# Mixture-of-experts layer: results stored in the lists' own order and fetched by index in the next layer's front, row scatters in pairs

## The chip, the cores and the metric

The kernel runs on one core of a Trainium2 chip. The metric is device microseconds (us) per execution. The kernel before takes 3396.26 us, the median of 10 runs (3391.55 to 3404.77).

The core's engines work in parallel, each on its own instruction stream: PE (TensorE, matrix products; PEld are its weight loads), DVE (VectorE), ACT (ScalarE), POOL (GpSimd) and SP (SyncE, which only issues DMAs). DMAs are issued by SP and ACT in hardware queues and by POOL in a software queue; the indirect ones, which take a row index per partition, are POOL's.

## The reference

The input is one image, 256 channels of 64 x 64, so N = 4096 tokens of C = 256 numbers. Four layers follow one another: two convolution-like ones, then two transformer layers, each attention and a mixture of experts. What the change touches is layer 2's experts (hidden size 256) and the attention of layer 3, cut here to its core:

```python
def _moe(tokens, router_w, w1, b1, w2, b2):          # layer 2, 8 experts, TOP_K = 2
    logits = tokens @ router_w.T
    probs = softmax(logits, axis=-1)
    rw, re = top_k(probs, TOP_K)
    rw = rw / maximum(rw.sum(-1, keepdims=True), 1e-12)
    combine = zeros((N, E)).at[arange(N)[:, None], re].set(rw)
    out = tokens
    for e in range(E):
        h = gelu(tokens @ w1[e] + b1[e])
        y = h @ w2[e] + b2[e]
        out = out + combine[:, e:e + 1] * y
    return out
```

Layer 3 is a softmax attention over all tokens with one head of 256 (on layer-normed tokens, in this kernel's form), then experts of hidden size 1024 with the same routing.

## The kernel before

**Tokens and lists.** The tokens lie in SBUF as a tile `t` of 32 token tiles of 128 tokens; four token tiles are a block (8 blocks). For each block the router (`route_parts`) norms the tokens, finds each token's two experts and weights (`top`, `exp`, `weigh`) and its place in each expert's list (`place`, `find`), and `scatter` (L2181) writes each token's row, 260 numbers, into the DRAM buffer `xs` at both places: two indirect DMAs on POOL per token tile. The row holds the normed token and four more numbers: the token's row index and its weights, which the experts use later.

**Expert tiles.** The lists are worked off in up to 39 tiles of 256 rows (`expert_tiles`), 36 always, the rest under an If (`expert_rest`, L2400/L2402). Tiles 0 to 12 (`FULL[2]` = 13) come from table A, which is known after six blocks are routed; table B orders the others. For one tile: SP loads the rows (`expert_rows`) and the expert's weights (`expert_weights`); PE turns the rows, and ACT or DVE copies them (`f_xT`, L2376/L2377); PE multiplies by the first matrix; ACT does the gelu (`f_h`, L2456); PE multiplies by the second; DVE adds the bias (`f_y`, L2534); ACT multiplies each row by its weight (L2536); and POOL scatters the 256 rows by two indirect DMAs (L2537) into the DRAM buffer `ys`, at the token's place for its first or second expert. `expert_where` works out weight and place with five or so small DVE operations.

**What is in which order.** The second layer's attention (`attn2_sum`, 16 steps u) and the tiles up to 12 are written in a fixed order per engine (`manual_schedule`); from tile 13 on the scheduler is free. In the attention the routing of block r is spread over the steps: `scatter` of its first two token tiles at one step, of the last two at the next, and POOL's other work there is `scale` (L1734), one operation per step. The routers of the last blocks (r5, r6, r7) end inside the expert tiles: a `plan` puts pieces of them at slots ("hs", "turn", "end") of tiles 0 to 9.

**Third layer's front.** After the experts, the products of the query and key weights (`a_w_ps`, L2705, L2708) are formed; for each block, two reads of `ys` (`outputs`, L2615) on SP's and ACT's queues, two adds into `t` (`add`, L2735), the statistics (`look`, L2742 to L2746), the norm on ACT (`norm`, L2755), the turn on PE (`turn`, L2766, L2768) and the product with the joint weight matrix (`ask`, L2779). Blocks 0 to 2 go ahead of the loop. The loop runs over steps g, for each query block one per 256 keys, so two per key block: `scores` (L2843, with sums on DVE, L2830 to L2848, and the exponential on ACT, L2862), sums of the exponentials (`a_et`, L2866 to L2868, on POOL for query block 0, on DVE later), `values` (L2882), and `fetch` (a load of keys and four sums of values on POOL, L2822 to L2825). Query block 0 starts before all keys are there: in its first twelve steps the even ones add block late + 1 and turn block late, and the odd ones look, ask and norm. PE's, POOL's and DVE's order is fixed there.

```python
for g in range(first):
    late = 2 + g // 2
    more = late + 1 < NBLK
    scores(g)
    (turn, ask)[g % 2](late, 0)
    if more:
        (add, look)[g % 2](late + 1)
    if g >= LAG:
        values(g - LAG)
```

Of the kernel before, what the change touches and what calls it, by code (L numbers as in the profile page):

```python
# [10 lines left out]
F32 = mybir.dt.float32  # L11
BF16 = mybir.dt.bfloat16
I32 = mybir.dt.int32
# [44 lines left out]
CX = C + 4  # L58

# [60 lines left out]
class Net:  # L120
# [1282 lines left out]
    def attn2(self, t, S):  # L1403

        nc, tc = self.nc, self.tc
        with tc.tile_pool(name="a2", bufs=1) as pool:
# [53 lines left out]
            ahead = lambda: self.expert_rows(self.xs, S["A"]["tab"], 0, x)  # L1460
            with left:
                at["wp"] = left.enter_context(tc.tile_pool(name="a2x", bufs=2))
                at["ps"] = left.enter_context(tc.tile_pool(name="a2x_ps", bufs=1, space=PSUM))
                r6, r7 = self.attn2_sum(t, A, tri, ked, at["wp"], at["ps"], route, late, self.list_tiles(S, lent, bank, "A"), ahead)
# [9 lines left out]
            put(0, r6["place"], r6["find"], r6["weigh"], lambda: r7["turn"](0))  # L1474
            put(1, lambda: r7["turn"](1, True), lambda: r6["scatter"](range(2)), lambda: r7["move"](range(TPB)))
            put(2, r7["logits"], lambda: r6["scatter"](range(2, TPB)))
            put(3, r7["top"], r7["exp"], r7["count"])
            put(4, r7["place"], r7["find"], r7["weigh"], lambda: r7["scatter"](range(2)))
            put(5, lambda: r7["scatter"](range(2, TPB)), go)
            put(6, go)  # L1480
            put(7, go)
            put(8, go)
            put(9, go)
# [5 lines left out]
        return tiles, on  # L1489
# [229 lines left out]
    def attn2_sum(self, t, A, tri, ked, wp, ps, route, late, lists, ahead):  # L1719
# [81 lines left out]
        with self.tc.manual_schedule(engines={ET.PE, ET.DVE, ET.Activation, ET.Pool}):  # L1801
# [4 lines left out]
            for u in range(U):  # L1806
                if u + 2 < U:
                    scale(u + 2)
# [8 lines left out]
                do(u, 4, "scatter", range(0, 2))  # L1817
                do(u, 5, "scatter", range(2, 4))
# [24 lines left out]
            r5["scatter"](range(2))  # L1843
# [8 lines left out]
            r5["scatter"](range(2, TPB))  # L1852
            r6["top"]()
            nc.scalar.activation(wp.tile([P, 1], F32, tag="g", name="f_gelu", bufs=1), self.one, AF.Gelu)
            r6["exp"]()
            r6["count"]()
        return r6, r7
# [196 lines left out]
    def clear_list(self, k, like, pool):  # L2054
# [4 lines left out]
        self.nc.sync.dma_start(out=part, in_=bc(zero.bitcast(F32), 1, N // P))  # L2059

    def top2(self, pool, lg, hot, w, e1):
# [6 lines left out]
        for r in range(2):  # L2068
# [8 lines left out]
            if r == 0:  # L2077
                nc.vector.tensor_scalar_add(e1, first, float(NE))
# [8 lines left out]
        def weigh():  # L2087
            nc.vector.tensor_scalar(w[:, 1], w[:, 0], -0.5, 0.5, ALU.mult, ALU.add)

# [13 lines left out]
    def route_parts(self, t0, T, t, S, wp, n, nT, bank):  # L2103
# [18 lines left out]
        def norm():  # L2122
            apply()
            nc.gpsimd.tensor_copy(n[:, :, C], self.out_row[:, tiles])
# [22 lines left out]
        def top():  # L2147
            hot = got["hot"] = room("f_hot", 2)[:, :, :T]
            got["exp"], got["weigh"] = self.top2(wp, got["lg"], hot, n[:, :, C + 1 : C + 3].rearrange("p i r -> p r i"), n[:, :, C + 3])
# [28 lines left out]
        def scatter(which):  # L2178
# [10 lines left out]
    def list_tiles(self, S, wp, bank, nm):  # L2189
# [66 lines left out]
        if not whole:  # L2256
            lines = 3
# [5 lines left out]
            nc.vector.tensor_tensor(last, self.nth[:, 0:1], last, ALU.is_le)  # L2263
# [9 lines left out]
        nc.vector.tensor_copy(T["tab"][:, 1, :n], p[:, 1])  # L2273
        nc.vector.tensor_copy(T["ex"][:, :n], p[:, 0])
# [14 lines left out]
    def tile_table(self, S, wp, bank):  # L2289
# [26 lines left out]
        tab = T["tab"][:, :, :n]  # L2316
        nc.vector.tensor_scalar_mul(tab[:, 0, :], ex, float(P))
# [6 lines left out]
        nc.vector.tensor_copy(tab[:, 1, :], skip)  # L2324
        rows = tl([NE], "rows")
        nc.vector.tensor_copy(rows, c_ps)
        nc.vector.tensor_copy(S["used"], ends[:, NE - 1 : NE])
# [5 lines left out]
        nc.vector.tensor_scalar(tau, self.count[:, :n], last, None, ALU.is_le)  # L2333
        nc.vector.tensor_mul(skip, skip, tau)
# [9 lines left out]
    def expert_rows(self, xs, tab, j, x):  # L2344
        row = self.expert_at(tab, 1, j, NE * N - MT)
        self.nc.sync.dma_start(out=x, in_=xs[bass.ds(row, MT), :].rearrange("(i p) c -> p i c", p=P))
        return x

# [9 lines left out]
    def expert_where(self, T, j, x, tl):  # L2358
        first, wgt, at = tl("first"), tl("wgt"), tl("at", I32)
# [46 lines left out]
    def expert_tiles(self, S, order, wp, ps, early, pre):  # L2406
# [14 lines left out]
        def rows(i):  # L2421
            if pre and i == 0:
                return pre["x"]

            return self.expert_rows(self.xs_parts[-1] if pre and L == 2 and 0 < i < FULL[2] else self.xs, *tab(i), wp.tile([P, NI, CX], F32, tag="x", name="f_x", bufs=ahead_x + 3))

        def weights(i):
            if given and i == 0:
# [6 lines left out]
                lambda: pool.tile([P, 2 * hidden + KH], F32, tag="w1", name="f_w1", **kw),  # L2435
# [3 lines left out]
        plan = dict(pre["plan"]) if pre else {}  # L2439
# [5 lines left out]
        def turn(x):  # L2445
            p = ps.tile([P, 2, MT], F32, tag="x", name="f_x_ps", bufs=1 if early else 2)
            return self.expert_turn(x, p, wp.tile([P, 2, MT], F32, tag="xT", name="f_xT", bufs=3), L == 2 and not free)

        def first(i, xT, w1, pairs):
            h = wp.tile([P, KH, MT], F32, tag="h", name="f_h", bufs=3)  # L2450

# [20 lines left out]
        def where(i, x):  # L2472
            tl = lambda tag, dt=F32: wp.tile([P, NI], dt, tag=tag, name="f_" + tag, bufs=8)
# [51 lines left out]
        def second(i, h, hs, w2, wt, at, wgt, beside=lambda: None):  # L2525
            y = wp.tile([P, NI, C], F32, tag="y", name="f_y", bufs=4 if L == 2 else 3)
# [3 lines left out]
            else:  # L2530
# [3 lines left out]
                nc.vector.tensor_tensor(y, p, bc(w2[:, KH * C :], 1, NI), ALU.add)  # L2534
# [10 lines left out]
        free = not pre  # L2545
        for i in tiles[:ahead_x]:
# [16 lines left out]
        for i in tiles:  # L2563
            if pre and i == pre.get("stop"):
                free = True
                written.close()
                yield
            if i + ahead_x <= tiles[-1]:
                xs[i + ahead_x] = rows(i + ahead_x)
# [721 lines left out]
```

## Time and profile before

| | |
|---|---|
| Median of 10 runs | 3396.26 us (3391.55 to 3404.77) |
| The profiled execution | 3394.9 us; its span 3393.1 us, mean granted TensorE clock 0.955 |
| PE, PEld | busy 3105.3 us (92%), 2326.0 us (69%) |
| DVE, ACT, POOL | busy 2266.4 us (67%), 1332.8 us (39%), 1464.2 us (43%) |
| L2181, row scatters to `xs`, one DMA | 64 of them, 1009 ns mean |
| L2537, result scatters to `ys`, one DMA | 144 in both expert layers, 1039 ns mean |
| HBM traffic | 287.07 MB read, 111.30 MB written |

Each group of instructions goes by its line (L2537), engine, operation and tiles (`out<-in`). A bracket such as [8.62 <-ACT f_xT L2377] is the time that the engine stood idle before the instruction, and the work that ended the wait; "issue" means that it waited for nothing that the profile shows. The granted clock is TensorE's, as a share of full speed. The durations come from one profiled execution.

### The profile page before, as it was taken

The page shows a single profiled execution, that of the slowest core. Times are in us where ns is not written, and L with a number is a line of the kernel's source. Part 1 is how long each engine was busy: PE and PEld are TensorE (multiplying, and loading weights), DVE is VectorE, ACT ScalarE, POOL GpSimd, SP SyncE. Part 2 cuts the span into 40 slices and gives each one's busy share as a digit, 9 for nine tenths or more (in the row PEclk, how much of TensorE's full clock was granted, in tenths as well). Part 3 has the DMA queues.
Part 4 walks back from the last instruction along what each step waited for, and adds up shares of the span by engine and source line. Part 5 has one row for each costly group of instructions (what it writes and reads, how often), then busy time and mean ns, then how long its engine had stood idle before and what let it go on. Part 6 is the DMA issues. An engine that isn't in the chain of part 4 may idle for free. (4 is left out here: it accounts for less than half of the span.)

```text
span 3393.1 us, 65702 instructions
## 1 busy us (share of the span) xinstructions
PE 3105.3 (92%) x25688; PEld 2326.0 (69%) x25688; DVE 2266.4 (67%) x5057; ACT 1332.8 (39%) x2569; POOL 1464.2 (43%) x1316
## 2 busy tenths in 40 slices
PE   6789999999977899797987979999999999999997
PEld 3343444344435888765766747888888888999997
DVE  8885677577764677787644475777777776555554
ACT  4444343434425666343443344222222222333332
POOL 2028787888852555434334444000000002655553
PEclk9889999999988999998878989999999999999998
DMA  1146555621134222200137754233323334555564
GB/s 72 40 108 151 161 153 156 153 61 52 50 106 124 64 75 75 58 1 2 39 121 229 239 204 167 81 100 97 103 87 94 100 94 148 192 213 203 211 245 166
DMA packets 241686, 406.99 MB, mean 120 GB/s; under 512 B 78353, under 2 KB 152850, under 8 KB 231890
## 3 DMA queue, kind: packets, MB, share of 16 engines
q1 hardware_dynamic: 212866, 347.55, 32.8%
q0 software_dynamic: 13056, 35.93, 2.8%
q10 hardware_dynamic: 15440, 19.16, 1.8%
q8 instruction: 207, 3.39, 0.4%
q14 instruction: 117, 0.96, 0.1%
HBM read 287.07 MB, written 111.30 MB: 117 GB/s over the span
## 5 line engine op out<-in xcount | busy, mean ns | idle before, releaser
L803 ACT COPY l_sc<-l_s 128x384 f32<-128x384 f32 (+1 forms) x632 | 304.0, 532 | 452.1 <-PE l_s L796 446.5
L808 DVE TENSOR_TENSOR l_sm<-l_s,mask 128x256 f32<-128x256 f32 (+2 forms) x628 | 307.8, 550 | 91.5 <-PE l_s L796 90.4
L179 PE MATMUL f_h_ps<-f_xT,f_w 128*128 128x256 f32 x1440 | 339.8, 387 | 29.6 <-ACT f_xT L2377 17.3
L2181 POOL DMA_INDIRECT xs<-f_room,f_to x64 | 64.6, 1009 | 644.5 <-DVE a_e L2830 477.1
L179 PEld LDWEIGHTS f_h_ps<-f_xT,f_w 128*128 128x128 f32 x1440 | 266.1, 192 | 80.6 <-ACT f_xT L2377 18.1
L796 PE MATMUL l_s<-l_q,l_k 32*128 32x256 f32 (+3 forms) x2944 | 270.5, 453 | 0.0
L2862 ACT ACTIVATE a_e<-a_e 128x512 f32<-128x512 f32 x256 | 156.0, 630 | 248.2 <-DVE a_e L2832 233.3
L813 POOL TENSOR_TENSOR l_sm<-l_sc,mask 128x768 f32<-128x768 f32 (+1 forms) x116 | 203.0, 1758 | 87.7 <-ACT l_sc L803 87.6
L2456 ACT ACTIVATE f_h<-f_h_ps,f_w 128x256 f32<-128x256 f32 x360 | 161.2, 470 | 174.9 <-PE f_h_ps L179 147.3
L1183 DVE TENSOR_TENSOR l_pr<-l_vk,l_w_ps 128x1280 f32<-128x1280 f32 x128 | 186.5, 1480 | 54.2 <-PE l_acc_ps L1187 35.1
L796 PEld LDWEIGHTS l_s<-l_q,l_k 32*128 32x128 f32 x2944 | 132.4, 183 | 115.2 <-issue 67.5
L1187 PE MATMUL l_acc_ps<-ident,l_pr 128*128 128x128 f32 x1600 | 198.1, 278 | 6.4 <-POOL l_pr L1178 6.2
L2537 POOL DMA_INDIRECT ys<-f_y,f_at x144 | 149.7, 1039 | 121.5 <-ACT f_y L2536 89.9
L1187 PEld LDWEIGHTS l_acc_ps<-ident,l_pr 128*128 128x128 f32 x1600 | 184.7, 144 | 13.1 <-POOL l_pr L1178 8.1
L817 POOL TENSOR_TENSOR l_sm<-l_sc,mask 128x256 f32<-128x256 f32 (+1 forms) x220 | 185.2, 872 | 14.0 <-ACT l_sc L803 13.2
L2484 POOL TENSOR_TENSOR f_wt<-f_w 128x512 f32<-128x512 f32 x72 | 95.9, 1344 | 213.3 <-PE f_ya_ps L179 184.1
L2843 PE MATMUL a_sa_ps<-a_q,a_kt 128*128 128x256 f32 x512 | 156.5, 387 | 16.7 <-DVE a_u L2848 15.2
L2847 ACT COPY a_u<-a_sa_ps 128x256 f32<-128x256 f32 x128 | 47.6, 372 | 293.2 <-PE a_sa_ps L2843 291.1
L842 PE MATMUL l_b_ps<-l_sm,l_v 128*32 128x256 f32 (+2 forms) x2176 | 153.4, 372 | 0.0
L2843 PE MATMUL a_sa_ps<-a_qt,a_kt 128*128 128x256 f32 x512 | 152.7, 380 | 0.0
L813 POOL TENSOR_TENSOR l_sm<-l_sc,mask_c 128x768 f32<-128x768 f32 (+1 forms) x64 | 122.3, 1928 | 37.2 <-ACT l_sc L803 36.8
L2882 PE MATMUL a_ob_ps<-a_et,a_vs 128*128 128x256 f32 x512 | 132.0, 380 | 0.0
(673 smaller groups left out, 7230.9 us busy)
## 6 DMA issues: line engine op xcount, KB each, us to landing
a_kt<-a_kd SPq DMA_DIRECT2D x128, 512.0 KB
f_w<-in_f_w SPq DMA_DIRECT2D x36, 1152.0 KB
f_w<-in_f_w SPq DMA_DIRECT2D x36, 1028.0 KB
xs<-zero SPq DMA_DIRECT2D x8, 4160.0 KB
l_vk<-vt SPq DMA_DIRECT2D x180, 128.0 KB
f_x<-xs SPq DMA_DIRECT2D x71, 260.0 KB
f_w<-in_f_w SPq DMA_DIRECT2D x36, 384.0 KB
l_rcp<-l_recd SPq DMA_DIRECT2D x48, 256.0 KB
```

The costliest lines, as they stand in the source:

```text
L179: self.nc.tensor.matmul(out, lhsT, rhs, start=(i == 0), stop=(i == len(pairs) - 1))
L796: nc.tensor.matmul(s[pair, j][:, at : at + m, :], key(hp), qs[hp], start=(z == 0), stop=(z == len(pieces) - 1))
L803: nc.scalar.copy(sc[:, j], s[1, j])
L808: nc.vector.tensor_tensor(to(pair, j, kind, at), pick(s[pair, j], kind, which), mask, ALU.mult)
L813: nc.gpsimd.tensor_tensor(out[:, :, at, :], of[:, :, which, :], bc(mask, 1, 2), ALU.mult)
L817: nc.gpsimd.tensor_tensor(to(1, j, kind, at), pick(sc[:, j], kind, which), mask, ALU.mult)
L842: nc.tensor.matmul(out, pieces[z][1](hp), self.halves(sms[pair][:, j], wide)[:, of + skip * lo : of + skip * (hi - 1) + 1 : skip], start=n ...
L1183: nc.vector.tensor_tensor(pr, vk, bc(held["w"][:, j, dy], 3, D), ALU.mult)
L1187: nc.tensor.matmul(acc[:, m, j, :], pf[:, dx, m * P : (m + 1) * P], self.ident, is_transpose=True, start=(j == 0 and dy == 0 and dx == 0 a ...
L2456: nc.scalar.activation(h[:, m, :], p[:, m % 2, :], AF.Gelu, bias=w1[:, 2 * hidden + m : 2 * hidden + m + 1])
L2843: mm = lambda out, i, right: nc.tensor.matmul(out, A[i], right, start=True, stop=True)
L2862: nc.scalar.activation(e[:, i : i + 3 : 2], e[:, i : i + 3 : 2], AF.Exp, scale=1.0 / 16.0)
```

## The change

- Layer 2's results are not weighted and not scattered. The tile `y` (128 x 2 x 260, its last four columns set to zero by POOL) is stored by one plain DMA of SP back into `xs`, at the rows it was read from. Rows are read and stored as "(p i)", two neighbouring rows to a partition. Tiles of the table that hold nothing read and store spare rows behind the lists, so `xs` is longer by 1792 rows, and clearing it has one more DMA. `expert_where` is gone for layer 2; the weights stay in SBUF (`S["wt"]`).
- `gather` fetches the two rows of each token of a token tile by two indirect DMAs on POOL, 1040 B a row; `take` multiplies by the weight and adds into `t` on DVE, two operations. Blocks 0 to 2 are gathered one token tile per expert tile in tiles 21 to 32, with take and statistics three tiles later; block 3 in tiles 33 to 36; the root (`root3`) and block 0's norm (`norm3`) are in tile 35. Blocks 4 to 7 are gathered in steps g = 0 to 7 of the third layer's loop, four indirect DMAs a step, and taken at the even steps.
- The row scatters of layer 2's attention are split in ones and twos of token tiles with the `scale` operations between them; those of r5's last three token tiles, r6's and r7's go to expert tiles 0 to 10, one token tile each, behind a one-element copy on POOL that reads that tile's `f_h` (`behind`). In layer 3's expert tiles 5 to 8 the last block's scatters also go one token tile each.
- The order of all 36 tiles is the written one. Weight loads are issued ahead of row loads; the rows of tile 13 (table B, which waits for all scatters) are asked at tile 11. The dummy gelu's output is in another pool.
- The weight products of the third layer are formed in tile 16; its attention weights are loaded there too.
- In the loop's first eight steps the even ones form `a_et` on DVE, the odd ones on POOL (before: POOL for all of query block 0).

The order of instructions on each engine shows besides that block 0's first turn stands ahead of the If on PE, and that POOL's order in the attention is two scatters, scale, four scatters, scale, two scatters per pair of steps.

```diff
 # attn2_sum
             for u in range(U):
-                if u + 2 < U:
+                do(u, 5, "scatter", [2])
+                if u % 2 and u + 2 < U:
                     scale(u + 2)
...
-                do(u, 4, "scatter", range(0, 2))
-                do(u, 5, "scatter", range(2, 4))
+                do(u, 4, "scatter", [0])
+                if u % 2 == 0 and u + 2 < U:
+                    scale(u + 2)
+                do(u, 4, "scatter", [1])
+                do(u, 5, "scatter", [3])
...
-            r5["scatter"](range(2))
+            r5["scatter"]([0])
...
-            r5["scatter"](range(2, TPB))
             r6["top"]()
-            nc.scalar.activation(wp.tile([P, 1], F32, tag="g", name="f_gelu", bufs=1), self.one, AF.Gelu)
+            nc.scalar.activation(lent.tile([P, 1], F32, tag="g", name="f_gelu", bufs=1), self.one, AF.Gelu)
 # attn2, plan of the expert tiles
-            put(1, lambda: r7["turn"](1, True), lambda: r6["scatter"](range(2)), lambda: r7["move"](range(TPB)))
+            send = lambda r, i: lambda: r["scatter"]([i], True)
+            put(1, lambda: r7["turn"](1, True), lambda: r7["move"](range(TPB)), send(r5, 2))
...
+            put(10, send(r7, 3))
 # expert_tiles
+        def behind():
+            nc.gpsimd.tensor_copy(wp.tile([P, 1], F32, tag="pulse", name="f_pulse", bufs=2), pulse["h"])
...
+                nc.gpsimd.memset(y[:, :, C:], 0.0)
+                nc.vector.tensor_tensor(y[:, :, :C], p, bc(w2[:, KH * C :], 1, NI), ALU.add)
+                where, k = order[i]
+                part = sum(k + (FULL[2] if where == "B" else 0) >= begun(2, b) for b in (2, 3)) if pre else 2
+                self.expert_store(part, S[where]["tab"], k, y)
+                return
...
             if pre and i == pre.get("stop"):
-                free = True
                 written.close()
                 yield
-            if i + ahead_x <= tiles[-1]:
-                xs[i + ahead_x] = rows(i + ahead_x)
+                written.enter_context(self.tc.manual_schedule(engines=pre["written"]))
             if i + ahead <= tiles[-1]:
                 ws[i + ahead] = weights(i + ahead)
+            most = FULL[2] - 1 if pre and L == 2 and i < FULL[2] - 2 else tiles[-1]
+            while asked <= min(i + ahead_x, most):
+                xs[asked] = rows(asked)
+                asked += 1
 # new
+    def expert_store(self, part, tab, j, y):
+        row = self.expert_at(tab, 1, j, NE * N + (NE - 2) * MT)
+        self.nc.sync.dma_start(out=self.yl_parts[part][bass.ds(row, MT), :].rearrange("(p i) c -> p i c", p=P), in_=y)
+    def gather(self, S, ti, y, xs):
+        for r in range(2):
+            self.nc.gpsimd.indirect_dma_start(out=y[:, r], in_=xs[: NE * N, :], out_offset=None,
+                                              in_offset=bass.IndirectOffsetOnAxis(ap=S["to"][:, r, ti : ti + 1], axis=0))
+    def take(self, S, t, ti, y):
+        for r in range(2):
+            self.nc.vector.scalar_tensor_tensor(t[:, ti, :], y[:, r, :C], S["wt"][:, r, ti : ti + 1], t[:, ti, :], ALU.mult, ALU.add)
 # attn3
+            also(FULL[2] + 3, "end", matrix)
+            for k in range((ahead + 1) * TPB):
+                i = begun(2, ahead - 1) + k
+                also(min(i, MOST), "end", lambda k=k, i=i: gather(*divmod(k, TPB), i < MOST))
+                if k < ahead * TPB:
+                    also(i + 3, "hs", lambda k=k: take(*divmod(k, TPB)), lambda k=k: look3(k))
+            also(MOST - 1, "turn", root3)
+            also(MOST - 1, "end", lambda: norm3(0))
...
                 def add(b):
-                    self.outputs(b, ys)
-                    part = t[:, b * TPB : (b + 1) * TPB, :]
-                    for y in ys:
-                        nc.vector.tensor_tensor(part, part, y, ALU.add)
+                    for i in range(TPB):
+                        take(b, i)
...
-                    eng = nc.gpsimd if b == 0 else nc.vector
+                    eng = nc.vector if b > 0 or g < 2 * (NBLK - ahead - 1) and g % 2 == 0 else nc.gpsimd
...
-                        fetch(g + 3)
+                        ask_for = lambda i, b=late + 2, g=g: b < NBLK and gather(b, 2 * (g % 2) + i)
+                        ask_for(0)
+                        fetch(g + 3, lambda: ask_for(1))
```

## The prediction, made before the changed kernel ran

> **What bounds the kernel now.** I first read the page: PE is busy 92% of the span, so time can only come from stretches where PE stands. The slices show such a stretch between 1700 and 1970 us, around the second layer's experts. I then cut that part into stages with the windows view; its columns are the window, busy us and instructions of PE, PEld, DVE, ACT, POOL, then granted clock, DMA share and GB/s.
>
> ```profile
> core 0: us, PE busy (x) PEld busy (x) DVE busy (x) ACT busy (x) POOL busy (x), PEclk, DMA share, GB/s
> 1617.89:1633.77 15.88, 15.55 (x246) 13.24 (x245) 12.62 (x43) 9.63 (x19) 0.00 (x0) 1.00 0.01 2
> 1633.77:1655.84 22.07, 20.80 (x245) 16.99 (x245) 14.13 (x43) 11.04 (x20) 10.23 (x11) 0.85 0.14 49
> 1763.17:1783.00 19.83, 19.60 (x100) 16.99 (x100) 4.18 (x21) 8.68 (x19) 8.31 (x9) 0.87 1.02 364
> 1783.00:1791.39 8.39, 0.00 (x1) 0.00 (x1) 0.64 (x5) 1.43 (x3) 4.86 (x5) 0.63 0.35 129
> 1811.80:1820.53 8.73, 0.03 (x1) 0.00 (x0) 3.02 (x13) 2.27 (x6) 3.88 (x4) 0.74 0.57 181
> 1820.53:1843.20 22.67, 22.67 (x103) 19.62 (x104) 10.18 (x65) 11.07 (x25) 9.72 (x10) 0.87 0.70 220
> 1941.70:1963.83 22.13, 3.57 (x17) 3.14 (x17) 9.54 (x23) 3.05 (x7) 3.77 (x4) 0.59 0.44 167
> 1963.83:1979.28 15.45, 13.61 (x33) 6.52 (x34) 9.37 (x23) 7.10 (x14) 4.00 (x8) 0.70 0.38 136
> 2008.48:2026.57 18.09, 16.65 (x74) 12.85 (x73) 13.17 (x30) 10.22 (x17) 9.09 (x15) 1.00 0.62 228
> ```
>
> The first two rows are two equal pairs of steps of the second layer's attention, without and with eight row scatters on POOL: 15.88 against 22.07 us. The next rows are expert tiles: PE is full while no burst runs, and stands 8.39 and 8.73 us after bursts of eight to ten indirect DMAs on POOL. 1941.70 is the end of the last second product; 22 us follow with 3.57 us of PE, then 15.45 us at clock 0.70. The last row is one period of two steps of the third layer's attention. The timeline names what is late (start, length, work, then idle before it and its releaser):
>
> ```profile
> 1788.35 0.97 POOL L2181 DMA_INDIRECT xs<-a_qk,f_to  x1 [0.30 <-issue]
> 1788.60 0.84 ACT L2456 ACTIVATE f_h<-f_h_ps,f_w 128x256 f32<-128x256 f32 x2 [9.73 <-issue]
> 1791.39 1.22 PE L179 MATMUL f_h_ps<-f_xT,f_w 128*128 128x256 f32 x2 [8.62 <-ACT f_xT L2377]
> ```
>
> PE waits for ACT's copy, but ACT itself stood 9.73 us on "issue", that is, on nothing that the profile shows, while POOL issued scatter after scatter, 0.97 + 0.30 us each. The same word stands at PE in the attention:
>
> ```profile
> 1658.81 0.97 POOL L2181 DMA_INDIRECT xs<-a_qk,f_to  x1 [0.30 <-issue]
> 1661.87 1.84 PE L1752 MATMUL a_s<-w_qkv,a_vT 32*128 32x128 f32 x22 [0.91 <-issue]
> ```
>
> So long runs of scatters hold the other engines' instruction streams. The Trainium skill, "Runtime: NRT & Kernel Launch", section "Instruction fetch mechanics", says that fetching is hidden by the rate at which a sequencer issues; by that rule the scatters have no such price and terms 1 and 2 below would fall to nearly nothing. The 9.73 us speak against it, and I go by them. At the layer's end the chain is plain:
>
> ```profile
> 1945.41 0.97 POOL L2537 DMA_INDIRECT ys<-f_y,f_at  x1 [0.30 <-DMA ys<-f_y,f_at]
> 1953.30 1.22 DVE L2735 TENSOR_TENSOR t<-t,a_e 128x1024 f32<-128x1024 f32 x1 [7.36 <-DMA a_e<-ys]
> 1956.78 1.22 DVE L2735 TENSOR_TENSOR t<-t,a_e 128x1024 f32<-128x1024 f32 x1 [1.86 <-DMA a_e<-ys]
> 1963.83 0.18 PEld L2766 LDWEIGHTS a_q_ps<-ident,a_vs 128*128 128x128 f32 x1 [16.46 <-ACT a_vs L2755]
> ```
>
> Last scatter, read of ys, two adds, norm, then PE.
>
> **Part by part.** All against the profiled execution, 3394.9 us (span 3393.1 and 1.8 around it), which lies 1.4 under the median.
>
> 1. *Scatters in the attention.* Four double steps carry eight scatters at 22.07 − 15.88 = 6.2 us extra each; the burst near 1726 to 1736 costs some 10. The change puts the scale between pairs, but in POOL's order it still reads two, scale, four, scale, two: the run of four stays, merely from other token tiles. Six scatters of the last burst leave for the expert tiles. I take 4 us gained, mostly from these. Ends: 2 lost (more switching) and 20 gained (if the runs of eight were the whole price).
>
> 2. *Expert tiles 0 to 12.* The first product starts at 1763.17. SP had waited 7.5 us on the dummy gelu before the first weight load; its tile now comes from another pool, and the copy on ACT is next late, near 1760.6. Tile 13 starts at 1843.2. The eleven token tiles still to be scattered (22 instructions) go two per expert tile, behind that tile's gelu. Two ys scatters per tile stood beside full PE in 1820.53 to 1843.20, so a pair costs PE nothing there. Then: 13 tiles at 3.9 us (written order, tiles 9 to 12) = 50.7, 5.2 of routing products, 6 for the cold clock and for the wait of tile 13's rows on the last scatters: 61.9, end 1822.5. Gain 20.7, call it 21. Ends: 8 (one of the two stalls stays, and a little more) and 26 (no cold clock).
>
> 3. *Tiles 13 to 35.* The written order costs 3.90 to 3.93 a tile, the free one 4.08 to 4.14. Removed per tile: two ACT multiplies, the weight lookups on DVE, two scatters; added: one store by SP, one POOL memset; and in tiles 21 to 32 two gathers on POOL (2 × 1.27 = 2.5 of 3.9 us), two DVE takes (0.43 each, by the 128x256 adds) and the statistics (0.57), hidden as DVE is half busy here. What may show is DMA: 656 KB of weights, 266 of rows, 266 stored, 266 gathered = 1454 KB, at 364 GB/s (above) 4.0 us. By the page's queues (q1 at 32.8% for 347.55 MB is 312 GB/s when full, q0 at 2.8% for 35.93 MB 378) it is 1188/312 + 266/378 = 4.5. So 8 tiles gain 1.2 to 1.5, 13 cost 0 to +6, and the moved matrix products add 2.6 plus a little. I take zero net, as 364 GB/s comes from this same stage; ends 6 gained, 8 lost. SP's new stores wait for DVE's bias add and stand ahead of later loads in its queue; these are asked two tiles ahead, so I give that nothing; without the cover it is in the 8.
>
> 4. *The front.* Before, first scores come 1979.28 − 1941.70 = 37.6 us after the last expert product. Now blocks 0 to 2 are fetched, added and their statistics done under tiles 21 to 35, and block 0 is normed there. What is left: the If's 2.2 us (PE stood 1941.7 to 1943.9) and the 15.45 of the row above, less half a turn (1.3) now ahead of the If and 1 to 2 for a warmer clock: 14.4 to 15.4. Gain 23 (18 if the clock drops as before and a late norm adds 2; 25 if it stays full).
>
> 5. *The third layer's loop.* Blocks 4 to 7 cost four gathers a step on POOL: 8 × 1.27 = 10.2 per period, on its 9.6, minus 2.2 of sums moved to DVE: 17.6 of 18.1, just under. DVE at the even step: score adds end 6.28 into the period, then before 2.44 us of adds to 8.7. Now the sums need the exponential (ends 8.46), take 1.45, and eight takes 3.4: DVE is free at 13.35, while the odd step's adds were due at 10.1. That is 3.2 us of PE wait in three periods and about 1 in the first, 10.8, plus some clock lost after each: 12 (2 if order slips past, 18 with POOL in the way). Everything hangs on the gathers' price on POOL. The scatters next to a DVE half busy took:
>
> ```profile
> L2537 POOL DMA_INDIRECT ys<-f_y,f_at x72: 966/972/999, 1774.3 to 1945.4; - x72
> ```
>
> Shortest, median and longest lie within 33 ns, so DVE does not delay them. The Trainium skill, "SBUF — State Buffer", section "A bandwidth-pool intuition that's wrong (but worth ruling out)", speaks against the change: a POOL-issued DMA of about 620 ns takes about 3100 beside a DVE copy. By that the loop's gathers would be 8 × 3.4 = 27 us a period, POOL would be the bound at 35, and four periods would lose about 68 us, estimated. This trace disagrees.
>
> Six rows at the last layer's end are spread likewise; PE is full there, so nothing. Clearing the spare rows is early, 1.9 MB in a quiet stretch: nothing; at 312 GB/s it would be 6 us.
>
> Sum: −4 − 21 + 0 − 23 + 12 = −36; 3396.3 − 36 = 3360.
>
> **Rivals.**
>
> *A, gathers starve PE as scatters do: slower.* 64 gathers at the attention's 6.2/8 = 0.77 us are 49 us; 49 − 36 = 13 slower, 3409. It decides from 0.56 us a gather. For it: same engine, same queue, and the loop has its gathers in fours. Against: 1820.53 to 1843.20, where scatters in pairs left PE at 22.67 of 22.67.
>
> *B, the gain moves into the loop.* Term 5 at 18 with 6 more of lost clock, and term 2 only 8: −4 − 8 − 23 + 24 = −11, 3385. For it: DVE already has 13.2 us of 18.1, and its order is fixed.
>
> *C, pairs do more than thought.* The attention falls to 15.9 us per double step: 20 instead of 4, 3344. Against: the run of four in POOL's order, which is also the case that the change does not do there what it says.
>
> **Numbers.** Forecast 0.55, A 0.17, B 0.20, C 0.08. The forecast's own bounds, not all at once, are about 3345 to 3376. The range must reach B and C and may leave most of A outside: 3334 to 3392. A measurement here tells about 0.2%, 7 us. Faster takes the forecast, C and nearly all of B: 0.79; within 0.2% 0.04; slower 0.17.
>
> **What would show it.** First scores about 15 us after the last expert product; no PE gap over 3 us in tiles 0 to 12; tile 13 near 1820; tiles 21 to 33 at 4.0 us; double steps of the attention still above 20 us; loop periods near 21 us with idle before the odd step's scores ended by DVE; gathers at about 1 us. Wrong if periods exceed 24 us, gathers take over 1.5 us, or "issue" gaps of several us appear beside the gathers.

## The result and the profile after

The changed kernel takes 3378.75 us (median of 8 runs, 3373.84 to 3387.18) against 3396.13 of the kernel before: a ratio of 0.9948, 95% interval 0.9939 to 0.9958. That is 17 us where 36 were forecast. The profiled execution has a span of 3377.2 us, 15.9 less than before (the rounded stages below add up to 16.0). All ratios compare fast runs; a run of 5633.98 us, the slowest of experiment 12, is left out of its ratio and median.

The stages of both traces, cut at the first or last matrix product of each kind, and the prediction's terms beside them:

| Stage | before, us | after, us | difference | forecast |
|---|---|---|---|---|
| start to the attention's first context product | 1590.8 | 1598.8 | +8.0 | 0 |
| context products of the second layer's attention | 158.0 | 151.5 | −6.5 | −4 |
| from there to expert tile 13 | 94.3 | 73.8 | −20.5 | −21 |
| tile 13 to the last expert product | 98.6 | 108.7 | +10.1 | 0 |
| last expert product to first scores | 37.6 | 17.9 | −19.7 | −23 |
| first 16 steps of the third layer's loop | 140.0 | 153.8 | +13.8 | +12 |
| the rest | 1273.8 | 1272.6 | −1.2 | 0 |

The windows of the changed kernel, columns as in the prediction:

```profile
1641.90:1664.20 22.30, 19.66 (x245) 15.44 (x244) 14.09 (x43) 11.03 (x20) 10.13 (x10) 0.85 0.14 49
1761.90:1782.70 20.80, 20.77 (x108) 18.27 (x109) 3.90 (x14) 8.28 (x18) 8.71 (x15) 0.90 0.80 283
1810.50:1824.10 13.60, 8.44 (x41) 6.62 (x40) 1.48 (x4) 2.74 (x6) 1.33 (x5) 1.00 0.78 259
1831.90:1847.10 15.20, 11.18 (x57) 8.99 (x56) 3.59 (x7) 2.74 (x6) 0.32 (x3) 1.00 0.87 284
1847.10:1878.30 31.20, 31.20 (x162) 27.53 (x162) 6.55 (x12) 10.53 (x24) 5.75 (x12) 1.00 0.76 248
1878.30:1927.50 49.20, 40.78 (x202) 33.61 (x202) 21.77 (x50) 13.82 (x30) 25.79 (x47) 1.00 0.91 307
1932.80:1950.70 17.90, 12.82 (x33) 6.15 (x33) 8.28 (x16) 11.14 (x20) 8.60 (x17) 0.81 0.50 174
1993.80:2016.80 23.00, 18.57 (x73) 13.39 (x72) 15.85 (x39) 11.02 (x19) 16.41 (x22) 0.93 0.55 177
```

The first tiles now keep PE full (20.77 of 20.80). PE stands in three places where it did not before: 5.2 us in tiles 11 and 12, 4.0 us in tiles 15 and 16, 8.4 us in tiles 25 to 34. In between, tiles 17 to 24 run at 3.9 us without a gap. The first 8 us lie in a layer that the prediction never looked at. There SP writes the zeros that clear `xs`, 4.2 MB at a time (a fill), and the new DMA for the spare rows stands behind the last fill. Before and after, the timeline shows:

```profile
593.78 0.58 SPq L2059 DMA_DIRECT2D xs<-zero  x1
595.09 11.71 SPq L873 DMA_DIRECT2D l_xs<-xd  x1
```

```profile
593.87 12.09 SPq L2072 DMA_DIRECT2D xs<-zero  x1
606.38 6.81 SPq L878 DMA_DIRECT2D l_xs<-xd  x1
645.58 1.67 PE L801 MATMUL l_s<-l_q,l_kc 32*128 32x384 f32 x8 [5.94 <-DMA l_kc<-l_k]
```

Whatever stands behind a fill holds SP for some 12 us: in the kernel before it was a load (11.71 us; 11.7 to 13.0 behind each of the eight fills), now it is the new zeros (12.09). What the new DMA adds is the 6.81 us that the load behind it is held in its turn, and every load after that comes later. In tiles 11 and 12 and in the loop the changed kernel shows:

```profile
1817.26 0.39 ACTq L162 DMA_DIRECT2D w_v3p<-in_w_v3p  x1
1817.83 0.84 ACT L2509 ACTIVATE f_h<-f_h_ps,f_w 128x256 f32<-128x256 f32 x2 [8.21 <-DVE f_y L2590]
1819.19 1.99 PE L184 MATMUL f_h_ps<-f_xT,f_w 128*128 128x256 f32 x8 [3.12 <-ACT f_xT L2421]
2003.21 4.11 DVE L2690 SCALAR_TENSOR_TENSOR t<-f_room,f_offB,t 128x256 f32<-128x256 f32 x8
2007.71 0.70 PE L2971 MATMUL a_sa_ps<-a_q,a_kt 128*128 128x256 f32 x2 [3.69 <-DVE a_u L2976]
2008.82 3.43 PE L184 MATMUL a_q_ps<-f_w,a_wqk 128*128 128x512 f32 x4
```

The last three lines are the forecast's term 5 as it was described: eight takes, then the odd step's sums, PE 3.69 us late, and its next four products at half speed (3.43; the same four took 1.88 a step later).

### The profile page after: what moved, and what is told of

It reads as the page before. It is cut to its first block, busy times and chain, and to the rows that moved or that the text cites. A ratio compares the mean times of both kernels' runs of the same rounds, so it can differ in the third digit from the quotient of the medians.

```text
span 3377.2 us, 65713 instructions
## 1 busy us (share of the span) xinstructions
PE 3092.4 (92%) x25688; PEld 2314.8 (69%) x25688; DVE 2249.1 (67%) x4885; ACT 1311.9 (39%) x2517; POOL 1450.6 (43%) x1350
## 5 line engine op out<-in xcount | busy, mean ns | idle before, releaser
L2201 POOL DMA_INDIRECT xs<-f_room,f_to x64 | 64.8, 1013 | 653.4 <-DVE a_e L2958 478.8
L184 PE MATMUL f_h_ps<-f_xT,f_w 128*128 128x256 f32 x1440 | 329.7, 382 | 8.6 <-ACT f_xT L2421 8.1
L822 POOL TENSOR_TENSOR l_sm<-l_sc,mask 128x256 f32<-128x256 f32 (+1 forms) x220 | 185.1, 869 | 15.1 <-ACT l_sc L808 14.2
L2971 PE MATMUL a_sb_ps<-a_qt,a_kt 128*128 128x256 f32 x512 | 131.4, 379 | 0.0
```

The source lines that it names most:

```text
L184: self.nc.tensor.matmul(out, lhsT, rhs, start=(i == 0), stop=(i == len(pairs) - 1))
L822: nc.gpsimd.tensor_tensor(to(1, j, kind, at), pick(sc[:, j], kind, which), mask, ALU.mult)
L2971: mm = lambda out, i, right: nc.tensor.matmul(out, A[i], right, start=True, stop=True)
```

## The experiments

Medians of one kernel differ by some us from one set of runs to the next (the kernel before: 3392 to 3398), so for parts of a few us the stages of the profiles decide, one execution each. The ratios to the kernel before say only whether the whole agrees. Those of experiments 1 to 5 (0.9942 to 0.9961) all overlap the changed kernel's 0.9948, so what their expectations say of the whole was neither seen nor ruled out; only the combinations at the end are clear of it.

**1. Weights later.**

```diff
-            self.weights(pool, ["w_qkT3", "w_v3p", "w_v3s"])
-            also(FULL[2] + 3, "end", matrix)
+            also(FULL[2] + 4, "end", lambda: self.weights(pool, ["w_qkT3", "w_v3p", "w_v3s"]))
+            also(FULL[2] + 7, "end", matrix)
```

> Only edit: the third layer's attention weights are loaded at the end of expert tile 17 instead of right after tile 12, and their products are formed at the end of tile 20 instead of 16. Theory (the moved load on ACT's queue waits for all row scatters and holds ACT's gelu behind it, and 1.0 MB more falls into a stretch where DMA is full): no ACT idle of 8 us before the gelu of tile 11, first products of tiles 11 to 18 take some 32 us instead of 40.6, and the whole is 6 to 9 us faster than the changed kernel. Rival (tile 13's rows, which wait for the last scatters, hold SP and so PE): tiles 11 to 13 keep their 13.6 us and the whole moves by less than 3 us.

Ratio 0.9961 (0.9949 to 0.9972). ACT's 8 us are gone, but from the start of tile 11 to that of tile 13 it is 14.2 us (13.6 without the edit): the rival holds.

```profile
1816.51 0.07 DVE L2176 MEMSET f_cum<- 128x8 f32 x1 [4.84 <-DMA xs<-a_qk,f_to]
1821.05 0.65 PE L2420 MATMUL f_x_ps<-ident,f_x 128*128 128x128 f32 x4 [4.29 <-DMA f_x<-xs]
```

The last scatters land at 1816.5, and only then tile 13's rows are read. Tiles 13 to 18 fall from 27.0 to 19.5 us, but tiles 18 to 25 rise from 27.2 to 34.8, where loads and products now are. Moving them moved their price: my theory was wrong, and the ACT wait was hidden behind another one. The last scatters are not all of that other wait: in experiments 11 and 12 they end with tile 8, and with SP's stores ahead of the loads (11) the two tiles still take 12.5 us, with the stores behind them (12) 8.3.

**2. Zeros spread.**

```diff
-        if k == NE - 1:
-            part = self.xs[NE * N :, :].rearrange("(p a) c -> p a c", p=P)
-            self.nc.sync.dma_start(out=part, in_=bc(zero.bitcast(F32), 1, (NE - 1) * NI))
+        rows = N + MT if k < NE - 1 else N
+        part = self.xs[k * (N + MT) : k * (N + MT) + rows, :].rearrange("(p a) c -> p a c", p=P)
...
```

> Only edit: the 1.9 MB of zeros for the spare rows are written in seven equal parts with the first seven list fills, instead of in one DMA of its own after the last. Theory (that DMA held SP's queue 12.1 us and so delayed the loads of the first layer's second half): the first score product of the second layer's attention starts some 8 us earlier, near 1591, and the whole is 7 to 9 us faster than the changed kernel. Rival (the 8 us before the second layer are a drift between executions): no change within 2 us.

Ratio 0.9942 (0.9923 to 0.9961). The first layer's last score product is at 980.6 instead of 989.9 (before: 981.0), the attention's first one at 1588.1 instead of 1594.7. The DMA was the cause: the load behind the last fill now holds SP for 11.76 us, as in the kernel before, with no second wait after it. The first of the two points lies between 985.6 and 989.9 in the eight kernels that keep the DMA (mean 987.1) and between 978.6 and 983.9 in the six without it (mean 981.1), so its price is some 6 us, and the 8.0 of the one profile is more than that mean.

**3. Stores behind the next loads.**

```diff
-                self.expert_store(part, S[where]["tab"], k, y)
+                stores.append(lambda: self.expert_store(part, S[where]["tab"], k, y))
 # in the loop, after the loads of tile i
+            flush()
```

> Only edit: SP's store of a tile's results is put behind the loads of the next tile instead of ahead of them. Theory A (the stores wait 44 us in all for the store before and for the bias add, and hold the loads behind them): the gaps that end with a row load in tiles 25 to 35 go, tiles 25 to 35 take 40 to 43 us instead of 49.2, the whole 5 to 8 us faster than the changed kernel. Theory B (DMA itself is the bound there: 68 us of packet time per tile over 16 engines is 4.3 us): tiles 25 to 35 still take 47 to 50 us and the whole moves by less than 2 us.

Ratio 0.9961 (0.9946 to 0.9977). From the start of tile 25 to that of tile 35 it is 46.2 us, between the two theories, and the front pays it back: 21.6 us to the first scores instead of 17.9. What is left in tile 25 showed the next suspect:

```profile
1877.94 0.95 POOL L2697 DMA_INDIRECT f_w<-xs,f_to  x1 [0.30 <-issue]
...
1880.48 0.84 ACT L2509 ACTIVATE f_h<-f_h_ps,f_w 128x256 f32<-128x256 f32 x2 [7.12 <-remote]
...
1881.85 3.42 PE L184 MATMUL f_h_ps<-f_xT,f_w 128*128 128x256 f32 x8 [3.84 <-ACT f_xT L2421]
```

Eight gathers in a row (1868.7 to 1878.9): by the code the first, which is written at tile 21, has to wait for the stores of the tiles before, and the paced ones behind it then ran without a pause.

**4. Takes two and two.**

```diff
-                    for i in range(TPB):
+                    for i in range(0 if b == ahead else 2, TPB):
                         take(b, i)
+                        if g % 2 == 1 and late + 2 < NBLK:
+                            take(late + 2, 0)
+                            take(late + 2, 1)
```

> Only edit: in the third layer's loop a block's four token tiles are taken two at the odd step before and two at the even step, instead of all four at the even step. Theory (DVE's eight takes stand before the odd step's score sums and PE waits 3.7 us for them, then runs at half clock): four products-to-products periods of two steps fall from 20.9, 22.2, 23.0, 23.7 us to some 19 to 20, and the whole is 7 to 11 us faster than the changed kernel. Rival (POOL's gathers, 17.6 us of work per period, are what sets it): periods stay above 21.5 us and the whole moves by less than 3 us.

Ratio 0.9944 (0.9927 to 0.9961). The periods:

```profile
1947.10:1967.80 20.70, 12.97 (x46) 8.36 (x45) 16.32 (x36) 5.67 (x10) 9.44 (x12) 0.92 0.48 179
1990.00:2009.70 19.70, 16.90 (x74) 12.74 (x73) 16.07 (x41) 10.37 (x18) 15.29 (x20) 1.00 0.60 188
2009.70:2029.20 19.50, 16.82 (x73) 12.71 (x72) 15.72 (x39) 10.18 (x18) 15.09 (x20) 1.00 0.55 190
```

The third and fourth fall from 23.0 and 23.7 to 19.7 and 19.5 us with the same gathers on POOL, clock 1.00; the first two, which take block 3 and the first half of block 4 more, stay at 20.7 and 22.2. Eight steps take 82.1 instead of 89.7 us. DVE's order made 7.6 of the loop's 13.8 us, and in these two periods the gathers on POOL were not the bound. With block 3's takes gone from the loop as well (experiment 11) the eight steps take 78.5.

**5. Gathers later.**

```diff
-                i = begun(2, ahead - 1) + k
+                i = begun(2, ahead - 1) + (2 + k - (k > 5) - (k > 9) if k < ahead * TPB else k)
```

> Only edit: the gathers of blocks 0 to 2 start at expert tile 23 instead of 21, two of the twelve token tiles doubling up with another (tiles 23 to 32). Theory (the first gather waits for the stores of the earlier tiles, and then eight run without a pause; they hold the other engines as the bursts of scatters do): no gap over 2 us in tiles 25 to 27, tiles 25 to 35 take 44 to 47 us instead of 49.2, the whole 2 to 5 us faster than the changed kernel. Rival (DMA's packets alone are the bound from tile 21 on): the gaps move along with the gathers and the sum of tiles 21 to 35 stays within 1.5 us.

Ratio 0.9957 (0.994 to 0.9973). Tiles 25, 26, 27 take 3.9, 4.6 and 3.9 us instead of 6.7, 5.6 and 4.6; tiles 25 to 35 take 45.2, and tiles 21 to 35 together 4.0 us less. The theory holds for the stage; in the kernels that leave the gathers and loads there alone, tiles 21 to 35 take 63.2 to 64.8 us, here 60.7. The gaps that remain end with a row load or stand behind runs of six gathers (experiment 9).

**6. The attention's old order.**

```diff
-                do(u, 5, "scatter", [2])
-                if u % 2 and u + 2 < U:
+                if u + 2 < U:
                     scale(u + 2)
...
-                do(u, 4, "scatter", [0])
-                if u % 2 == 0 and u + 2 < U:
-                    scale(u + 2)
-                do(u, 4, "scatter", [1])
-                do(u, 5, "scatter", [3])
+                do(u, 4, "scatter", range(0, 2))
+                do(u, 5, "scatter", range(2, 4))
```

> Only edit: in the second layer's attention the row scatters stand as in the kernel before (two token tiles at one step, two at the next, the scale ahead of them); all else as changed. Theory of the prediction (the order of POOL is worth some 4 us there, and the rest of the 6.5 us that this stage gained comes from the burst that left its end): the stage from first to last context product takes 153 to 156 us instead of 151.5. Rival (the pairs are worth all of it): 158 us as before. Other rival (the order is worth nothing): 151.5.

Ratio 0.9976 (0.9965 to 0.9986). The stage takes 159.8 us: the order of POOL is worth all of its gain, 8.3 us. Any two steps in a row, from the first with scatters on (six overlapping pairs of steps), take 23.1 to 23.4 us in the old order, four scatters, scale, four scatters, scale, and 19.3 to 22.3 in the new one, two, scale, four, scale, two. The edit moves the scale along with the scatters, so the runs do not say whether the shorter runs gained this or the place of the scale.

**7. The tiles' old bursts.**

```diff
-            put(1, lambda: r7["turn"](1, True), lambda: r7["move"](range(TPB)), send(r5, 2))
-            put(2, r7["logits"], send(r5, 3))
+            put(1, lambda: r7["turn"](1, True), lambda: r6["scatter"](range(2)), lambda: r7["move"](range(TPB)))
+            put(2, r7["logits"], lambda: r6["scatter"](range(2, TPB)))
...
```

> Only edit: the scatters of the last eleven token tiles stand where they were in the kernel before: three at the end of the attention, four at the ends of expert tiles 1 and 2, four at those of tiles 4 and 5, without the copy that paces them. Theory (bursts of eight scatters hold the streams of PE, ACT and DVE for 8 to 9 us each): two gaps of 6 to 9 us in tiles 2 to 9, tile 11 starts 60 to 68 us after tile 0 instead of 48.6. Rival (the stalls came from the weight lookups and result scatters between them, which are gone): tile 11 starts within 52 us of tile 0.

Ratio 0.9967 (0.9953 to 0.9982). Tile 11 starts 51.9 us after tile 0, tile 13 62.4 us after it (changed kernel: 48.6 and 62.2). The theory falls: in the changed kernel the bursts cost 3.3 us, and since they end earlier, tile 13's rows come earlier by nearly as much (tiles 11 to 13 in 10.5 us instead of 13.6).

**8. The other half of that square.** The kernel before, with the paced scatters alone:

```diff
-            put(1, lambda: r7["turn"](1, True), lambda: r6["scatter"](range(2)), lambda: r7["move"](range(TPB)))
+            send = lambda r, i: lambda: (self.behind(), r["scatter"]([i]))
+            put(1, lambda: r7["turn"](1, True), lambda: r7["move"](range(TPB)), send(r5, 2))
...
```

> The kernel before with one edit: the last eleven token tiles' scatters go one token tile per expert tile in tiles 0 to 10, paced as in the changed kernel; its result scatters, weight lookups and the attention stay. Theory of the prediction (bursts make the two 8 us stalls): tile 11 starts 50 to 56 us after tile 0 instead of 72.1, and the whole is 10 to 18 us faster than the kernel before. Rival, from the run with bursts but no result scatters (51.9 us): the result scatters and lookups are what has to go, and tile 11 still starts over 62 us after tile 0.

Ratio 0.9986 (0.9976 to 0.9996). Tile 11 starts 68.8 us after tile 0. The four cases: bursts in the kernel before 72.1, pairs in it 68.8, bursts in the changed kernel 51.9, pairs in it 48.6. Pacing is worth 3.3 us either way; all else that the change did to these tiles 20.2. That is the going of the result scatters together with that of the weight lookups on DVE and the multiplies on ACT, and the new order of loads; no run takes these apart. What speaks for the result scatters is what pairs became in the kernel before:

```profile
1780.73 0.97 POOL L2182 DMA_INDIRECT xs<-a_qk,f_to  x1 [0.30 <-issue]
1783.27 0.84 ACT L2466 ACTIVATE f_h<-f_h_ps,f_w 128x256 f32<-128x256 f32 x2 [7.03 <-remote]
1784.64 1.65 PE L179 MATMUL f_h_ps<-f_xT,f_w 128*128 128x256 f32 x3 [4.50 <-ACT f_xT L2378]
```

Four indirect DMAs a tile are 5.1 us, a tile is 3.9: POOL hardly pauses, and row scatters and result scatters join into runs of eight (1771.7 to 1781.7) and even twelve (1805.7 to 1820.9, PE idle for 6.3 us behind it).

**9. Less to move.** The kernel of experiment 5, tiles 26 to 35 without weight loads:

```diff
+            if not (pre and L == 2 and i > 25):
+                kept["w"] = weights_at(i)
+            return kept["w"]
```

> The kernel of the later gathers, and tiles 26 to 35 use the weights that tile 25 loaded, so that 0.66 of 1.45 MB per tile is not moved (their products are those of another expert: this part of the computation is changed). Theory (after the burst is gone, DMA's packets are the bound where gathers run): tiles 26 to 35 at 3.9 us each, tiles 25 to 35 take 39 to 40.5 us instead of 45.2. Rival (SP's order, with stores ahead of loads, is what makes the rows late): still 43 us or more.

This variant ran once. Tiles 25 to 35 take 42.4 us instead of 45.2, so both parts of the dispute are half right. All of them but two run at 3.9 to 4.0 us: there the weight loads had been in the way, by their packets (DMA share 0.63 instead of 0.87 over 1878.3 to 1927.5) or by their places in SP's queue, which the edit empties as well. Tiles 30 and 33 take 5.5 us, both after a run of six gathers (where two token tiles share an expert tile); the first:

```profile
1898.12 0.95 POOL L2692 DMA_INDIRECT f_w<-xs,f_to  x1 [0.30 <-issue]
...
1900.19 0.84 ACT L2516 ACTIVATE f_h<-f_h_ps,f_w 128x256 f32<-128x256 f32 x2 [4.73 <-PE f_y_ps L184]
...
1901.56 1.78 PE L184 MATMUL f_h_ps<-f_xT,f_w 128*128 128x256 f32 x7 [1.47 <-ACT f_xT L2421]
```

**10 to 12. Together.** Experiments 1 to 5 in one, with the products spread over four tiles and the scatters ending with tile 8; the same with the stores ahead of the loads again and block 3's takes in the front; and that with only the first twenty tiles' stores behind:

```diff
+            for k in range(4):
+                also(FULL[2] + 7 + k, "end", lambda k=k: matrix(*divmod(k, 2)))
 # front, second and third
+                    take(3, 0)
+                    take(3, 1)
                     query(0)
 # third
+                if not pre or i >= 20:
+                    flush()
```

> The changed kernel with all of these: attention weights loaded at tile 17 and their products spread over the ends of tiles 20 to 23, the zeros of the spare rows spread over seven fills, stores behind the next tile's loads, takes two and two, gathers from tile 23, and the last scatters ending with expert tile 8 instead of 10. If the causes add up: 8 (fill) + 8 (takes) + 4 to 7 (weights and products) + 5 to 8 (gathers and stores) + 4 to 6 (tile 13's rows) = 29 to 37 us under the changed kernel, 0.984 to 0.987 of the kernel before. If DMA is the bound in tiles 21 to 35, some 7 less.

> As the combination before, but SP's stores stay ahead of the next loads (putting them behind gained 3 us in tiles 25 to 35 and lost 4 in the front), and block 3's takes stand in the front between the asks and turns instead of in the first step of the loop. By the parts: fill 8, tile 13's rows 4, weights and products 3, gathers 4, takes 8 and front takes 2 to 5: some 29 us under the changed kernel's profiled 3377 span, 3346 to 3355, ratio to the kernel before 0.985 to 0.989. If the loop's first periods stay at 20 us, the front takes are worth nothing.

> The second combination with one more edit: the stores of tiles 0 to 19 stand behind the next tile's loads, those from tile 20 on ahead of them. Theory (SP's order is what delays tile 13's rows and the tiles near the attention weights' load, while at the end late stores only hold up the front): tiles 11 to 13 take 8 to 10 us instead of 12.5, the front stays within 0.5 us, and the whole is 2 to 5 us under the second combination, 0.986 to 0.988 of the kernel before. Rival (DMA is full there and the order is worth nothing): no change within 1 us.

Ratios 0.9901 (0.9884 to 0.9917), 0.9889 (0.987 to 0.9909) and 0.9892 (0.9874 to 0.9911): medians 3360.78, 3357.5 and 3356.8 us. All beat both kernels. The first gained half of what was added up and missed its range: tiles 13 to 35 still take 99.0 us (103.4 changed), with 5 us of it now in tiles 18 to 25, where loads and products were put, and the front takes 2 us more. The second is inside its expected ratio and 2.5 us over its expected time, the loop's eight steps now 78.5 us. The third does what was expected where it was expected (tiles 11 to 13 in 8.3 us instead of 12.5), but not 2 to 5 us in the whole, which is the second's within the interval, and its ratio is above the range expected.

## Why the prediction was right or wrong

36 us were forecast and 16 came in the profile. Two terms that the prediction set to nothing make 18 of the 20 us between: tiles 13 to 35 (10.1) and the zeros (8.0). The other misses nearly cancel.

**Term 1, the attention: right sign, undersized, and for another reason.** The order was read rightly: the run of four stays in POOL's order. But the prediction took that to mean that little was to be gained from the order, and most from the scatters that leave the last burst. Experiment 6 gives all of it, 8.3 us, to the order, run of four and all.

**Term 2, first tiles: right size, by luck.** 61.9 us were forecast from tile 0 to 13, 62.2 measured. The sum explains the gain by the pairs that replace bursts, and those are worth 3.3 us; the rest of the change to these tiles, which the sum did not count as a gain, is worth 20.2 of 23.5 us to tile 11. And the wait for tile 13's rows, forecast within 6 us together with the cold clock, took 5.8 alone (13.6 us for tiles 11 and 12, against 7.8 before): the pacing that gained 3.3 us moved the last scatter later and lost it again there (experiment 7). The bursts themselves were misread: by the trace they are not eight to ten indirect DMAs but twelve, 1774.3 to 1789.3 and 1799.1 to 1814.1.

**Term 3, the step that failed: zero taken, 10.1 measured.** It had three holes. The moved load was counted as products, not as DMAs: 1.0 MB where DMA was already 0.93 busy (1843.2 to 1863.0 us of the kernel before), one of the loads in ACT's queue with an 8 us wait (hidden behind that for tile 13's rows, experiment 1). The products took 4.9 us, not 2.6, as each waits for DVE's copy of the one before (in window 1831.90 to 1847.10, which also has 2.35 us of PE waiting for a row load). And of the two DMA prices, 4.0 and 4.5 us a tile, I took the nearer row's; tiles 25 to 34 took 4.9, against 3.9 without a gap: 0.3 of it goes with the weight loads (2.8 us of ten tiles, experiment 9), about 0.4 with the run of gathers that the first one's wait for the stores set off (4.0 us, experiment 5). That wait was not in the prediction. The 4.0 us are net of the two new runs of six in that experiment, which cost 1.6 us each (experiment 9); with these added back, the 0.3 that is left would be the run's too, as an estimate. SP's stores ahead of the loads were given nothing; behind the loads they are worth 3 us in tiles 25 to 34, lost again in the front (experiment 3), and 4 us at tile 13 (experiments 11 and 12).

**The zeros, the second step that failed: nothing taken, 8.0 measured.** "A quiet stretch" was said without a row: in the kernel before, SP's queue already stood 11.71 us behind the last fill there. The price by bytes that the prediction gave and set aside, 6 us, is what the DMA costs: 6.81 us of SP's queue, and some 6 us at the end of the first layer over the kernels with and without it.

**Term 4, the front: 3.3 short.** The clock was expected warmer: the row says 0.81, but the first eight ask products ran at half speed (6.19 us against 3.70 a little later), and the If took 2.69, not 2.2.

**Term 5, the loop: right** in place and, for the larger part, in cause, and 13.8 against 12. Splitting the takes gives back 7.6 of it (experiment 4), block 3's takes another 3.6 (experiment 11). A take's operation costs 484 ns (median), not 430, and the clock fell in three of the four periods (0.92, 0.93 and 0.86).

**The rivals.** A was decided at 0.56 us a gather: in the loop and in paced tiles gathers cost PE far less, but unpaced they do hold the others, and A's mechanism made 4 us of term 3. The prediction's sign for it came in one place: an idle ACT beside the gathers of tile 25. B's 3385 came nearer to the result than the forecast, for reasons that it did not name: the loop took 13.8, not 24. C's mechanism, pairs doing more than thought, was there at less than half of its size.

**What holds the others.** The prediction reads "issue" as the other engines' instruction streams being held, and so as evidence against the Trainium skill, "Runtime: NRT & Kernel Launch", section "Instruction fetch mechanics". The kept trace of the kernel before does not bear that out. In the 9.73 us ACT already had its next instruction, a wait for a semaphore; the longest of its line is that one:

```profile
L2456 ACTq EVENT_SEMAPHORE x36: 17/134/10695, 1763.1 to 1937.1; - x36
```

From 1776 to 1791.4 us the DMA view lists packets of the queues q1 and q0 alone, none of q8 and q14, which the profile's page marks as instruction queues. And in the trace's semaphore records the counter that PE's products raise moves at 1788.53 us, 7.9 us after the modelled end of the products that ACT waits for (1780.60); ACT starts 0.07 us later. In experiments 3, 8 and 9 the same signal is 4.7, 5.3 and 2.2 us late behind the runs of eight, eight and six. So what came late is PE's signal, or the end of its products, of which the profile only has a model; the rule on fetching is not contradicted here, and why a run of indirect DMAs delays the signal stays open.

On the shared port (the Trainium skill, "SBUF — State Buffer", "A bandwidth-pool intuition that's wrong (but worth ruling out)") the gathers beside a DVE that was busy 0.6 of the time (0.74 in the loop's first eight steps) show:

```profile
L2685 POOL DMA_INDIRECT f_w<-xs,f_to x40: 949/962/1062, 1872.0 to 2018.3; - x40
L2685 POOL DMA_INDIRECT f_room<-xs,f_to x24: 947/962/1192, 1920.7 to 2041.7; - x24
```

At most 1192 ns, not 3100. But DVE's work beside them was additions, multiply-adds and statistics; no copy, of which the page speaks, ran beside a gather in this trace. So the loop's price of 68 us did not come, and the page's sentence is not refuted by it, as "this trace disagrees" had it.

## What to carry to other kernels

Of every DMA that a change adds or moves, write down the queue, what it waits for and what stands behind it, beside its bytes: tile 13's rows and the first gather were such waits, and the zeros cost the time of their bytes because loads stood behind them. When two mechanisms are removed together (here bursts and the rest of the old tiles' work), the size of the gain does not tell which one made it; the square of four runs does, as far as its two sides are single things. A load moved within a stretch where DMA is nearly full kept its price (7.5 us in tiles 13 to 18, 7.6 in tiles 18 to 25, experiment 1).

## What was not expected of the hardware

The price of a run of indirect DMAs on POOL grew with its unbroken length: in these tiles PE lost 1.5 us after runs of six (experiment 9), 1.0 to 4.5 after runs of eight (3, 7 and 8), 6.3, 8.6 and 8.7 after runs of twelve (experiment 8 and the kernel before); pairs with a pause cost nothing that shows. And whatever DMA is issued right behind a fill of 4.2 MB on SP's queue holds SP for 12 us (11.7 to 13.0 behind the eight fills of the kernel before), though the fill itself takes 0.6. Why a run of indirect DMAs makes the signals between PE and the others late stays open.
